# A window-attention and linear-attention kernel: chunks of 128 tokens in time order instead of 112, the image kept by rows

## The chip, the cores and the metric

The kernel runs on one NeuronCore of a Trainium2 chip. The metric is the device time of one execution in microseconds. Before the change it is 1951.62 us, the median of three runs (1951.55 to 1955.96). A profile of one execution stands beside it: every instruction with its start, its duration and what it waited for.

## What is computed

The input is a batch of 16 images of 56 x 56 positions and 128 channels, in fp32. It passes through three layers, each added to its input; the reference, cut to what matters:

```python
# layer 0: attention inside shifted windows of 7 x 7, 4 heads of 32 channels
x = roll(groupnorm(x), (-3, -3));  q, k, v = split(x @ w_qkv);  windows of 49 tokens
attn = softmax(q @ k.T * scale + bias + mask);  x = x0 + roll((attn @ v) @ w_out + b_out, (3, 3))
# layer 1: linear attention over the 3136 tokens of an image in order of time
q, k, v = split(layernorm(t) @ W.T + b);  q = elu(q) + 1;  k = elu(k) + 1
num = einsum('bti,btij->btj', q, cumsum(k[..., None] * v))
den = einsum('bti,bti->bt', q, cumsum(k));   t = t + num / (den + 1e-6)
# layer 2: batch norm of layernorm(t) @ W.T over all 16 images, then a recurrence along the tokens
y = sigmoid(wx_t + y @ V.T);   t = t + y
```

The sum over earlier tokens in layer 1 is computed by chunks: inside a chunk by a masked product of queries and keys (`A`), across chunks by a running state of 128 x 129 (keys by values, with a column of ones for the denominator).

## The kernel before

**Order of the work.** The first part of the program, layers 0 and 1, is written as a list of steps. Each has an engine, an assumed cost, a rank, the steps that it follows, and the buffers that it takes and drops (class `Plan`, lines 58 to 207). When the program is built, the planner plays the list against the assumed costs, first by rank and then up to thirty times by latest start, keeps the best and emits the steps in order of their planned starts. Each engine then executes its own instructions strictly in the emitted order. The numbers of buffers of each kind stand in the dictionary at line 433: three PSUM banks `b`, two pairs of banks `a`, two each of `xn`, `xnT`, `f0`, `f1` and `k`, one `A`, three `state`.

**Tiling.** Tokens lie on partitions in chunks of two image rows, `CH` = 112 tokens; an image has `NCH` = 28 chunks, worked on in `NG` = 7 groups of `G` = 4. Because the windows are shifted by three columns, a row is stored in shifted order: columns 3 to 50, then 51 to 55, then 0 to 2 (`ROW_PIECES`). A load or a store of a group therefore is six DMAs on SyncE's queue (lines 269 and 908), and the causal mask comes from the host in the permuted order of time.

**Layer 0.** `turned` (line 542) loads the groups of one image and transposes them to channels on partitions (L540). ScalarE copies the result into `xw_buf`, where each window's 49 tokens lie together (L567); VectorE takes the statistics (L577). A small chain gives the normalised weights `ws` (L598 to L628; L633 is its last product, once an image). `window_row` (line 672) handles a row of eight windows, eight of them an image: projections of queries and keys (L686) and values (L713) straight from `xw_buf`, scores (L737), softmax on VectorE, GpSimd and ScalarE (L748 to L782), transposes (L792), the product with the values (L811), and ScalarE's copy into `oT_buf` (L832), in token order with shifted rows.

**Layer 1.** `token_group` (line 927) handles a group of four chunks: bias (L937, GpSimd), output projection of layer 0 (L949), addition (L958), layer norm (L871 on VectorE, L878 to L890 on GpSimd), transposes (L540) and copy (L978), features of keys and queries (L991, then L1001, L1010 on ScalarE and L1014 on VectorE), values (L1035, L1044), transposed keys (L1058, L1062), products of keys and queries (L1072) with the mask (L1082). For each chunk follow the products with the state (L1101) and with `A` (L1104), the state's update (L1112) and its copy (L1124). Then come the division and addition (L1172 to L1179), the store (L918), a second layer norm, and the input of the recurrence (L1195, L1199), with batch statistics (L1202) and a copy into `staged` (L1210). `staged` is written to DRAM by sixteen DMAs an image (line 1231).

**Layer 2.** The last part runs the recurrence for 28 segments of 112 steps in parallel, 128 lanes of channels and 16 images, after a warm-up of 16 steps (L1438, L1450, L1453), transposes the results (L1487), adds the layer's input (L1496) and stores the output (L1502). Its inputs come back from DRAM in blocks of eight steps; the last image's part is copied from `staged` by GpSimd (L303). The change leaves this part as it is, apart from that copy.

Of the kernel before, what the change touches and what calls it, by code (L numbers as in the profile page):

```python
# [9 lines left out]
F32 = mybir.dt.float32  # L10
# [4 lines left out]
WS = 7  # L15
# [3 lines left out]

ROW_PIECES = ((0, 3, 48), (48, 51, 5), (53, 0, 3))
# [188 lines left out]
def tile_conv_attn_hybrid(  # L211
# [24 lines left out]
    NCH = T // CH  # L236
    G = 4
    NG = NCH // G
# [24 lines left out]
    xw_bufs = [hold.tile([P, NU, NW, 64], F32, name=f"xw_buf{i}") for i in range(2)]  # L263
    oT_buf0 = hold.tile([P, NU, NW, 64], F32, name="oT_buf0")
# [4 lines left out]
    def load_pieces(b, xt, c0, c1, engines):  # L269

        part = x[b].rearrange("(c r) w ch -> r w c ch", r=2)
        i = 0
        for r in range(2):
            for j, col, n in ROW_PIECES:
                engines[i % len(engines)].dma_start(
                    xt[W * r + j : W * r + j + n, c0:c1], part[r, col : col + n, c0:c1]
                )
                i += 1

    def time_cuts(t0):  # L280

        if t0 < 0:
            return ((0, W + t0, -t0), (-t0, 0, KB + t0))
        return ((0, t0, KB),)
# [10 lines left out]
    def last_xs(to, m):  # L295

        part = to.rearrange("p n c -> p (n c)").rearrange(
            "p (b k n) -> p b k n", b=B, k=KB
        )[:, B - 1]
        row, t0 = divmod(m, W // KB)  # L300
        t0 = KB * t0 - DISP
        for k0, p0, n in time_cuts(t0):
            nc.gpsimd.tensor_copy(  # L303
                part[:, k0 : k0 + n], staged[:, W * row + p0 : W * row + p0 + n, :]
            )
# [30 lines left out]

    FIRST = ((0, G), (G, 3 * G), (3 * G, NCH))
    for c0, c1 in FIRST:
        load_pieces(0, xt_bufs[0], c0, c1, (nc.sync, nc.scalar))
# [14 lines left out]
    bout_sb = constant("bout_sb", [CH, C], b_out.partition_broadcast(CH))  # L354
    awT_sb = constant("awT_sb", [P, 3 * P], attn_wT)
    bqk_sb = constant("bqk_sb", [P, 2], attn_b[0 : 2 * C].rearrange("(i p) -> p i", p=P))
    bv_sb = constant("bv_sb", [CH, C], attn_b[2 * C : 3 * C].partition_broadcast(CH))
    fwT_sb = constant("fwT_sb", [P, P], ffn_wT)
    causal_sb = constant("causal_sb", [CH, CH], causal)
# [10 lines left out]
    with ExitStack() as s1:  # L370
# [40 lines left out]

        q_bufs = []
# [6 lines left out]
        for i in range(2):  # L419
            vb = keep.tile([CH, G, C + 1], F32, name=f"v_buf{i}")  # L420
# [4 lines left out]

        nc.gpsimd.memset(xw_bufs[0][..., WT:], 0.0)
# [3 lines left out]
            xw_bufs[1].rearrange("p u w k -> p (u w k)")[:, 0 : PADQ * CH * C // P],  # L430
# [16 lines left out]
                "xnT": 2,  # L447
                "xfT": 1,
                "r": 1,
                "f0": 2,  # L450
# [1205 lines left out]
```

## Time and profile before

| | |
|---|---|
| median of three runs | 1951.62 us |
| the profiled execution, time | 1951.62 us |
| its span, first to last instruction | 1949.8 us |
| granted TensorE clock, mean over the span | 0.988 |
| last matmul of layers 0 and 1 (L1199) starts at | 1745.8 us |
| DMA: packets, bytes | 164993, 161.25 MB |
| packets under 512 B | 20001 |

The profile names TensorE's matmuls PE and its weight loads PEld (they overlap), VectorE DVE, ScalarE ACT, GpSimd POOL and SyncE SP. L686 is line 686 of the kernel; in the changed kernel lines have other numbers. A matmul in fp32 is two records in the trace (a transpose is one). Durations of matmuls overlap, since they are pipelined, so their sum isn't the time that they take; the distance from one start to the next is nearer to it. "Idle before" of an instruction is the time in which its engine stood still ahead of it, and the releaser is what ended last before it started.

### The profile page before, as it was taken

To read this page: it belongs to the slowest core of one execution; us is meant where nothing else is said; L and a number is where in the kernel's file an instruction comes from. 1 tells how busy PE (TensorE), PEld (TensorE's weight loads), DVE (VectorE), ACT (ScalarE), POOL (GpSimd) and SP (SyncE) were. 2 spreads that over 40 slices of the span, in tenths; PEclk is the share of its full clock that TensorE was granted. 3 is DMA by queue.
4 is the path that set the end of the run, shared out by engine and by line. 5 is a ranking of instruction groups with operands and counts; after the bars stand their busy time and mean duration, and the time that the engine had idled before them with its cause. 6 is when DMAs were issued, how large, how long until landed. Compare 5 with 4: busy or idle time off the path is not lost.

```text
span 1949.8 us, 68357 instructions
## 1 busy us (share of the span) xinstructions
PE 1866.5 (96%) x27854; PEld 1547.4 (79%) x27854; DVE 1370.3 (70%) x3243; ACT 1267.5 (65%) x2755; POOL 1192.9 (61%) x1992
## 2 busy tenths in 40 slices
PE   5999999999999999999999999999999999989787
PEld 4788888888888888888888878888888888767676
DVE  4767767676777767677677677766777767668677
ACT  3767666666666666666766667666766666547455
POOL 5767758676666768576766667676867656640000
PEclk9999999999999999999999999999999999989889
DMA  4112111121212121111212121212111121545998
GB/s 128 33 35 64 26 46 53 40 61 33 64 35 68 26 68 35 55 36 40 64 31 69 37 62 28 68 33 64 31 50 35 29 75 35 198 150 198 413 400 292
DMA packets 164993, 161.25 MB, mean 83 GB/s; under 512 B 20001, under 2 KB 148737, under 8 KB 162881
## 3 DMA queue, kind: packets, MB, share of 16 engines
q1 hardware_dynamic: 163032, 156.02, 25.1%
q8 instruction: 221, 3.62, 0.8%
q10 hardware_dynamic: 1640, 0.80, 0.2%
q14 instruction: 100, 0.81, 0.2%
HBM read 80.38 MB, written 76.38 MB: 80 GB/s over the span
## 4 chain that ended last, share of the span: by engine, by line
PE 82%; DVE 6%; DMA 5%; ACT 3%; issue 2%; POOL 2%; SPq 0%; DVEq 0%; POOLq 0%; ACTq 0%
PE bank L991 9%; PE bank L686 8%; PE bank L540 6%; PE bank L713 6%; PE state_bank L1112 5%; PE pair L737 5%; PE pair L1101 5%; PE bank L1035 5%; PE pair L1104 5%; PE pair L792 5%; PE bank L949 5%; PE pair L811 4%; PE bank L1072 4%; PE bank L1199 4%; DMA out_dram<-o_a 3%; PE bank L1058 2%
## 5 line engine op out<-in xcount | busy, mean ns | idle before, releaser
L782 POOL TENSOR_TENSOR p_buf<-p_buf,rc 128x784 f32<-128x784 f32 x128 | 194.4, 1519 | 127.0 <-DVE rc L779 83.7
L763 POOL TENSOR_TENSOR s<-s,mx 128x784 f32<-128x784 f32 x128 | 192.3, 1502 | 96.0 <-DVE mx L760 89.1
L686 PE MATMUL bank<-xw_buf,ws 128*128 128x392 f32 x512 | 215.2, 507 | 3.8 <-ACT xw_buf L567 1.4
L991 PE MATMUL bank<-xnT,awc_sb 128*128 128x448 f32 x448 | 210.0, 551 | 2.4 <-DVE xt_buf L958 0.7
L1001 ACT ACTIVATE r<-bank,bqk_neg 128x448 f32<-128x448 f32 x224 | 142.2, 635 | 102.6 <-PE bank L991 81.4
L1014 DVE SCALAR_TENSOR_TENSOR f<-bank,bqk_one,r 128x448 f32<-128x448 f32 x224 | 150.3, 671 | 65.3 <-ACT r L1010 64.6
L748 DVE TENSOR_TENSOR s<-pair,wmask_sb 128x784 f32<-128x784 f32 x128 | 123.7, 966 | 87.4 <-PE pair L737 77.7
L1112 PE MATMUL state_bank<-v_buf,k 112*128 112x129 f32 x864 | 174.0, 283 | 2.4 <-ACT k L1062 1.9
L1104 PE MATMUL pair<-v_buf,A 112*112 112x129 f32 x896 | 172.8, 273 | 0.2
L1124 ACT COPY state<-state_bank 128x129 f32<-128x129 f32 x432 | 117.5, 272 | 82.5 <-PE state_bank L1112 77.5
L1101 PE MATMUL pair<-state,f 128*112 128x129 f32 x864 | 169.8, 278 | 0.0
L1112 PEld LDWEIGHTS state_bank<-v_buf,k 112*128 112x128 f32 x864 | 137.6, 190 | 39.4 <-issue 18.3
L1101 PEld LDWEIGHTS pair<-state,f 128*112 128x112 f32 x864 | 129.9, 176 | 46.4 <-issue 35.2
L937 POOL TENSOR_TENSOR xt_buf<-xt_buf,bout_sb 112x512 f32<-112x512 f32 x112 | 141.8, 1279 | 18.2 <-DMA awT_sb<-in_attn_wT_dram 11.2
L777 DVE TENSOR_REDUCE sm<-p_buf 128x16 f32<-128x784 f32 x128 | 122.9, 960 | 41.3 <-ACT p_buf L773 40.5
L802 ACT COPY pT<-pair 128x904 f32<-128x904 f32 x128 | 118.0, 922 | 48.3 <-PE pair L792 44.9
L1453 ACT ACTIVATE y_a<-z_buf,bsh 128x224 f32<-128x224 f32 x224 | 100.1, 447 | 67.5 <-PE z_buf L1450 66.6
L713 PE MATMUL bank<-ws,xw_buf 128*128 128x128 f32 x1024 | 137.6, 277 | 0.0
L713 PEld LDWEIGHTS bank<-ws,xw_buf 128*128 128x128 f32 x1024 | 126.1, 191 | 10.1 <-issue 5.6
L1010 ACT ACTIVATE r<-r 128x448 f32<-128x448 f32 x224 | 130.3, 582 | 2.7
L1179 DVE SCALAR_TENSOR_TENSOR xt_buf<-pair,rd,xt_buf 112x128 f32<-112x128 f32 x448 | 125.5, 342 | 7.3 <-POOL lrs_a L884 0.5
L1104 PEld LDWEIGHTS pair<-v_buf,A 112*112 112x112 f32 x896 | 128.8, 177 | 1.5 <-DVE A L1082 0.8
(143 smaller groups left out, 4897.2 us busy)
## 6 DMA issues: line engine op xcount, KB each, us to landing
out_dram<-o_a SPq DMA_DIRECT2D x13, 1792.0 KB
x_d<-xt_buf SPq DMA_DIRECT2D x224, 96.0 KB
xt_buf<-in_x_dram SPq DMA_DIRECT2D x211, 96.0 KB
xs_d<-staged SPq DMA_DIRECT2D x180, 112.0 KB
xw_buf<-x_d SPq DMA_DIRECT2D x8, 2048.0 KB
spare<-xs_d SPq DMA_DIRECT2D x4, 1680.0 KB
oT_buf<-x_d SPq DMA_DIRECT2D x3, 2048.0 KB
xs_ring<-xs_d SPq DMA_DIRECT2D x3, 1680.0 KB
```

What stands on the lines that cost most here:

```text
L686: nc.tensor.matmul(d[key], o["ws"][:, j * P : (j + 1) * P], xk, start=True, stop=True)
L713: nc.tensor.matmul(d["pv"][:, w2, :], o["xw"][:, u, 2 * w2 : 2 * w2 + 2, :].rearrange("p w k -> p (w k)"), o["ws"][:, 2 * P : 3 * P], star ...
L763: nc.gpsimd.tensor_tensor(d["sf"], d["sf"], d["mx"].unsqueeze(2).to_broadcast([P, nb, WT]), ALU.subtract,)
L782: nc.gpsimd.tensor_tensor(prf, prf, d["rc"].unsqueeze(2).to_broadcast([P, nb, WT]), ALU.mult)
L937: nc.gpsimd.tensor_tensor(t["xt"][:, sl, :], t["xt"][:, sl, :], bout_sb.unsqueeze(1).to_broadcast([CH, G, C]), ALU.add,)
L991: nc.tensor.matmul(d[f"p{j}"], awc_sb[:, j * P : (j + 1) * P], d["xnT"].rearrange("p c t -> p (c t)"), start=True, stop=True,)
L1001: nc.scalar.activation(d[f"r{j}"], d[f"p{j}"], AF.Relu, bias=bqk_neg[:, j : j + 1], scale=-1.0,)
L1010: nc.scalar.activation(d[f"r{j}"], d[f"r{j}"], AF.Exp, scale=-1.0)
L1014: nc.vector.scalar_tensor_tensor(d[key].rearrange("p c t -> p (c t)"), d[f"p{j}"], bqk_one[:, j : j + 1], d[f"r{j}"], ALU.add, ALU.max,)
L1101: nc.tensor.matmul(to, d["f0"][:, cc, :], t["states"][c], start=True, stop=False)
L1104: nc.tensor.matmul(to, d["A"][:, cc, :], v1[:, cc, :], start=c == 0, stop=True)
L1112: nc.tensor.matmul(t["pd"], d["k"][:, cc, :], v1[:, cc, :], start=c == 0, stop=True, skip_group_check=True,)
```

## The change

- Chunks are 128 tokens in plain time order, 24 of them and one of 64. There are still seven groups: six of four chunks, and one with the chunk of 64. The recurrence keeps its 28 segments of 112 steps.
- A group's load or store is one DMA over 128 partitions; the write of `staged` is one DMA an image instead of sixteen. The causal mask is made on GpSimd.
- The image on channels is kept by rows, unshifted, 59 columns by 59 rows: ScalarE copies whole rows and the cut pieces at a group's ends, and GpSimd repeats the first three columns and rows at the far sides (`again`).
- VectorE copies each row of windows from there into one of two small buffers (`gather_windows`), and the projections read that. The second of them lies in the unused end of `oT_buf`.
- The attention's output is written unshifted, so ScalarE cuts the last window of each row in two (`mix_out`: four pieces for a row of windows, eight for the one that wraps, where there were two and four). The copy into `staged` is cut where segments of 112 begin.
- `xnT`, `f0` and `f1` have one buffer instead of two. The assumed costs of the steps are set for the new sizes, and the projections L949 of successive groups are put in order.

The diff, cut to its core (line numbers left out; a line of "..." stands for what is left out):

```diff
+    CK = P
     G = 4
-    NG = NCH // G
+    GT = G * CK
+    GROUPS = [(t0, [CK] * G) for t0 in range(0, T - GT + 1, GT)]
+    GROUPS.append((T // GT * GT, [T % GT]))
+    NG = len(GROUPS)
+    SIDE = H + DISP
...
+    def load_group(b, xt, g, engine):
+        engine.dma_start(
+            chunks_of(g, xt), tokens_of(g, x[b].rearrange("h w c -> (h w) c"))
+        )
...
-    FIRST = ((0, G), (G, 3 * G), (3 * G, NCH))
-    for c0, c1 in FIRST:
-        load_pieces(0, xt_bufs[0], c0, c1, (nc.sync, nc.scalar))
+    for g in range(NG):
+        load_group(0, xt_bufs[0], g, nc.scalar if g % 2 else nc.sync)
...
-                "xnT": 2,
+                "xnT": 1,
...
-                "f0": 2,
-                "f1": 2,
+                "f0": 1,
+                "f1": 1,
...
                 def copy(g=g):
...
+                    xw = image_rows(xw_buf)
+                    t0, t1 = group_tokens(g)
+                    at = t0
+                    while at < t1:
+                        y, c = divmod(at, W)
+                        m = 0 if c else (t1 - at) // W
+                        n = m * W if m else min(W - c, t1 - at)
+                        src = o[g][:, at - t0 : at - t0 + n]
+                        if m:
+                            src = src.rearrange("p (y c) -> p y c", y=m)
+                            nc.scalar.copy(xw[:, y : y + m, 0:W], src)
+                        else:
+                            nc.scalar.copy(xw[:, y, c : c + n], src)
+                        at += n
...
+            def again():
+                xw = image_rows(xw_buf)
+                nc.gpsimd.tensor_copy(xw[:, 0:H, W:SIDE], xw[:, 0:H, 0:DISP])
+                nc.gpsimd.tensor_copy(xw[:, H:SIDE, :], xw[:, 0:DISP, :])
...
+            def gather_windows():
+                y = DISP + WS * u
+                d["xk"] = x_bufs[i % 2]
+                nc.vector.tensor_copy(
+                    d["xk"][:, :, 0:WT].rearrange("p w (i j) -> p w i j", i=WS),
+                    image_rows(xw_buf)[:, y : y + WS, DISP:SIDE].rearrange(
+                        "p i (w j) -> p w i j", w=NW
+                    ),
+                )
...
-                    for i0, y0, m in row_parts(u):
-                        nc.scalar.activation(
-                            rows[:, par, :, y0 : y0 + m],
-                            src[:, :, i0 : i0 + m],
-                            AF.Identity,
-                            bias=o["bias"][:, 2:3],
-                        )
+                    for i0, y0, m in row_parts(u):
+                        at, ys = slice(i0, i0 + m), slice(y0, y0 + m)
+                        pieces = [(rows[:, 0, :, ys], src[:, :, at])]
+                        if par:
+                            cut = WS - DISP
+                            pieces = [
+                                (rows[:, 1, 0:last, ys], src[:, 0:last, at]),
+                                (rows[:, 1, last, ys, 0:cut], src[:, last, at, 0:cut]),
+                                (first[:, ys, 0:DISP], src[:, last, at, cut:WS]),
+                            ]
+                        for to, piece in pieces:
+                            nc.scalar.activation(
+                                to, piece, AF.Identity, bias=o["bias"][:, 2:3]
+                            )
...
+            xk = st("DVE", (0.45, 0.53), rank, gather_windows, [*taken, last_value[i % 2]], drops=[xw_buf])
-            pq = st("PE", (0.67, 0.83), rank, lambda: proj(0, "pq", bq), [*normed, last_score[i % 2]], takes=[bq])
+            pq = st("PE", (0.67, 0.83), rank, lambda: proj(0, "pq", bq), [xk, *normed, last_score[i % 2]], takes=[bq])
...
             def project():
-                d["po"] = bank(bo, CH, G, C)
-                oTf = t["oT"].rearrange("p y w -> p (y w)")
-                for cc in range(G):
-                    c = G * g + cc
+                d["po"] = bank(bo, np, nk, C)
+                for cc in range(nk):
                     nc.tensor.matmul(
                         d["po"][:, cc, :],
-                        oTf[:, c * CH : (c + 1) * CH],
+                        t["oT"][:, t0 + np * cc : t0 + np * (cc + 1)],
                         wout_sb,
                         start=True,
                         stop=True,
                     )
...
+            if g < NG - 1:
+                s = st("PE", (0.44, 0.61), rank, turn_k, [fk], takes=[bk], drops=[bfk])
+                ko = st("ACT", (0.48, 0.59), rank, k_out, [s], takes=[k], drops=[bk])
...
             def xs_out():
...
-                nc.scalar.copy(
-                    t["xsT"][:, :, sl], d["pw"].rearrange("p c j -> p j c")
-                )
+                at = t0
+                while at < t1:
+                    n, j = divmod(at, CH)
+                    m = 0 if j else (t1 - at) // CH
+                    size = m * CH if m else min(CH - j, t1 - at)
+                    src = d["pw"][:, at - t0 : at - t0 + size]
+                    if m:
+                        to = t["xsT"][:, :, n : n + m]
+                        src = src.rearrange("p (n j) -> p j n", n=m)
+                    else:
+                        to = t["xsT"][:, j : j + size, n]
+                    nc.scalar.copy(to, src)
+                    at += size
...
-                for r in range(2):
-                    for m in range(W // KB):
-
-                        for k0, p0, n in time_cuts(KB * m - DISP):
-                            nc.sync.dma_start(
-                                xs_d[r * (W // KB) + m, :, b, k0 : k0 + n, :],
-                                t["xsT"][:, W * r + p0 : W * r + p0 + n, :],
-                            )
+                nc.sync.dma_start(
+                    xs_d[:, :, b].rearrange("m p k n -> p m (k n)"),
+                    t["xsT"].rearrange("p (m k) n -> p m (k n)", k=KB),
+                )
```

## The prediction

> **What bounds the kernel now.** I read the page first, then the busy time by stretches of the span, then who TensorE waited for, then TensorE's instructions in order of time. The page and the stretches:
>
> ```profile
> span 1949.8 us, 68357 instructions
> PE 1866.5 (96%) x27854; PEld 1547.4 (79%) x27854; DVE 1370.3 (70%) x3243; ACT 1267.5 (65%) x2755; POOL 1192.9 (61%) x1992
> ...
> PEclk9999999999999999999999999999999999989889
> ```
>
> ```profile
> 20.00:50.00 30.00, 22.06 (x342) 16.50 (x343) 13.65 (x26) 11.78 (x25) 18.57 (x19) 1.00 0.37 112
> ...
> 1150.00:1250.00 100.00, 98.87 (x1631) 83.06 (x1633) 72.61 (x177) 68.55 (x148) 71.48 (x116) 1.00 0.17 49
> ...
> 1800.00:1850.00 50.00, 37.66 (x222) 32.08 (x220) 33.57 (x56) 25.27 (x57) 1.31 (x4) 0.90 1.02 412
> ```
>
> The columns are length, then busy PE, PEld, DVE, ACT, POOL, granted clock, DMA share, GB/s. Three stages show. Until about 29 us the first image is loaded and normalised. From there to 1746 us (the last L1199 starts at 1745.8) the sixteen images go through attention and linear attention: TensorE is busy 98 to 99% at clock 1.00, the others near 70%, the DMAs at 17%. The last 204 us are the recurrence, where the output's DMAs are full; its instructions are the same in the changed kernel. So the middle stage decides, and the question there is whether "99% busy" means no slack. The waits of TensorE between 400 and 1600 us say yes:
>
> ```profile
> PE state_bank L1112 <- ACT k L1062: 1.2, 2, 0.8
> PE bank L540 <- DVE gst L577: 1.0, 2, 0.6
> PE bank L686 <- DVE v_buf L1044: 0.9, 1, 0.9
> ```
>
> These are the three longest of a list that sums to some 13 us in 1200. TensorE waits for nobody: the stage lasts as long as its instructions take to issue. One image takes (1598.9 - 426.7)/11 = 106.6 us, by the starts of L633, which runs once an image. What one step costs is the distance from its start to the next start, not its duration (durations overlap):
>
> ```profile
> 660.59 0.92 PE L991 MATMUL bank<-xnT,awc_sb 128*128 128x448 f32 x2
> 661.34 0.38 PE L1101 MATMUL pair<-state,f 128*112 128x129 f32 x2
> 661.56 0.39 PE L1104 MATMUL pair<-v_buf,A 112*112 112x129 f32 x2
> 661.78 0.60 PE L1058 MATMUL bank<-ident,f 128*112 128x128 f32 x4
> 662.22 1.06 PE L713 MATMUL bank<-ws,xw_buf 128*128 128x128 f32 x8
> 663.11 0.94 PE L792 MATMUL pair<-ident,p_buf 113*128 113x113 f32 x8
> 663.89 0.40 PE L1112 MATMUL state_bank<-v_buf,k 112*128 112x129 f32 x2
> 664.12 1.04 PE L949 MATMUL bank<-wout_sb,oT_buf 128*112 128x128 f32 x8
> 665.00 0.55 PE L540 MATMUL bank<-ident,xn 112*128 112x112 f32 x4
> 665.38 0.95 PE L1072 MATMUL bank<-f,f 128*112 128x112 f32 x8
> 666.17 0.40 PE L1112 MATMUL state_bank<-v_buf,k 112*128 112x129 f32 x2
> ```
>
> L991 takes 0.75 us; one L1101, L1104 or L1112 takes 0.22; a step of four takes 0.44 (L1058), 0.89 (L713), 0.88 (L949, and L1035 likewise at 672.30), 0.38 (L540), 0.79 (L1072). The cost goes with the columns of the moving operand: 128 columns cost 0.22 whether the stationary operand has 112 (L949) or 128 (L713).
>
> **TensorE's work, step by step.** An image has 3136 tokens: 28 chunks of 112 before, 24 of 128 and one of 64 after. Where the tokens are the moving operand, the columns stay 3136 and the cost stays: L991 and L1199 7 x 0.755 = 5.29 against 6 x 0.863 + 0.12 = 5.30 each; the three transposes 7 x 0.385 = 2.70 against 6 x 0.44 + 0.06; L1072 5.50 against 5.45. Where the chunk is stationary or summed over, each chunk pays its own 128 or 129 moving columns, and three chunks fewer pay (per image):
> - L949 and L1035: 28 x 0.2195 = 6.15 to 24 x 0.2225 + 0.22 = 5.56, -0.59 each
> - L1058: four fewer (the last chunk leaves no state), -0.44
> - L1101 and L1104: three fewer of each, -1.32; L1112: three fewer, -0.67
>
> The sum is -3.61 us. The chunk of 64 brings some eight steps of 0.06 to 0.2 us of its own; for switching to them I add 0.2. So -3.4 us an image, -54.6 us in all. The instruction order of the changed kernel has these counts: 384 + 16 of L949's kind, 384 of L1112's.
>
> Here a rule speaks against the change. The Trainium skill, "TensorE: Matmul & The Clock Gate", section "LDWEIGHTS (loading the stationary operand)", says that a weight load takes its columns divided by 1.2 GHz, and its Part 3 ("What overlaps and what doesn't") that a load overlaps running matmuls only in other row groups. By that the wider chunk would lengthen each of 120 matmuls an image (project, values, products, attends) by two loads of 16 more columns, 2 x 13.3 ns: 3.2 us, nearly all of the gain. The rows say otherwise: 0.2225 against 0.2195, 3 ns; and the L540 transposes, with 128 stationary columns, follow each other every 95 ns, which is less than the rule's 107 for the load alone. I take the rows.
>
> **What moves to the other engines** (per image, the busy shares of the stretch above times 106.6 us as the base):
> - VectorE gathers the windows, 8 copies of 392 columns. The trace has no such copy. The nearest row is L1551, 448 columns contiguous, 382 ns; at the rate of L1561 (432 columns, two inputs, 597 ns) it would be 0.56. So 2.8 to 4.5 us; I take 0.45 each, 3.6. Fewer chunks give back 3 x 0.342 (L1179), 6 x 0.277 (L871) and about 0.9 (L958, L1044): -3.6. Below nothing it can't go. VectorE stays at 76 us.
> - ScalarE writes the image by rows (19 pieces, not 14), the staged inputs (18, not 7) and the attention's output (36, not 18): 34 more instructions for the same columns. L567's rows, 224 ns for 56 columns and 536 for 392, give 172 ns for an empty piece; in sequence pieces overlap, and two of 392 and 56 together took 0.59, so about 0.06. That is 2.0 to 5.8 us, less 3 x 0.272 (L1124) and 0.585 (L1062): +0.6 to +4.4 on 73. I take +2.5, since most pieces follow one another directly.
> - GpSimd copies the wrapped rows and columns (0.6 to 0.7 by L303, 224 columns 0.37), and saves about 3.2 on the small group's L937, L890 and L884: 72 us.
> - SyncE issues one DMA where there were six (L275, L918; six took 2.73 us) and one for the sixteen pieces of an image's staged inputs. Its queue was waiting for VectorE most of the time anyway: nothing.
>
> At 103 us an image all three stand at 70 to 75% beside TensorE, so I cost them at nothing but the waits that they cause. Cover: about 27 us an image of free time on each. What can be late is a hand-over in a full queue. TensorE's waits were about 1.2 us an image; I add 0.25 for a busier ScalarE and for the gather ahead of each row's projections: +4 us (bounds 0 and 25).
>
> Three buffers go from two to one (xnT, f0, f1). f0 is held until a group's last attend, so the next group's maximum (L1014), products (L1072) and mask (L1082) follow it in series: 0.74 + 0.89 + 0.69 and hops, 2.7 us, behind attends of about 2.8 us. That is 5.5 of 14.7 us a group. In the changed order TensorE has 4.4 us of other work (median, priced as above) between a last attend and the next products, and under 1 us in 2 of 111 cases. Nothing is late there.
>
> At the start, 18 issues of 0.64 to 0.76 us on two queues become 7, all of them over 128 partitions, and the last group is small. Stage one ends with GpSimd's seven L937 from 17.5 to 26.9 us ahead of the small power; with their bias earlier it may end up to 6 us sooner, or 1 us later by the wrap copy. I take -3. The end, where the small group follows the last full one through a chain of 9 us: +1.
>
> Sum: 1949.8 - 54.6 + 4 - 3 + 1 = 1897.2 us span, and with the 1.8 us outside the span 1899 us. The profiled execution's 1951.62 is the median itself.
>
> **Rivals.**
> - *ScalarE is late* (0.13): its 34 pieces cost the full 172 ns and land ahead of copies that free TensorE's three PSUM banks. For: three banks, and L567 and L1210 hold one through all pieces. Against: 75% is no bound. Waits of 2 to 3.5 us an image, 1915 to 1945, say 1925.
> - *The weight load is the pace* (0.03): the rule above; 0.2 to 0.4 us an image stay, about 1946, no change.
> - *Slower: the single f0 buffer* (0.05). Place: from the last L1104 through L1014 and L1072 to the next L1104. It decides if VectorE's and TensorE's queues add so much that TensorE stands over 0.5 us in each of 112 hand-overs (112 x 0.5 eats the gain); at 0.8 us it gives about 1899 + 85 = 1985. Against it the 4.4 us of cover.
>
> **How the numbers follow.** The likeliest case (0.79) is 1899 us, from 1885 (no added waits, start -6, the small chunk's switching free) to 1913. The range 1885 to 1922 takes in half of the ScalarE case. Under 0.3% (5.9 us) a measurement of this kernel can't tell from no change. Faster by more: 0.79 + 0.13 = 0.92; within: 0.03; slower: 0.05.
>
> **What would show it.** Right: L633's starts 103 us apart; L949's kind at 0.89 per four with 400 in all; TensorE's waits under 2 us an image; ScalarE under 76% in the middle stage; the last 204 us unchanged. Wrong: waits of TensorE on L1014's successor or on the pieces of L567 and L1210, or a step of 128-column chunks above 0.95.

## The result and the profile after

The changed kernel takes 1936.38 us (median of 4 runs, 1933.64 to 1937.03) against 1953.40 for the kernel before on the same chip (1951.55 to 1955.96). The ratio is 0.9909, 95% interval 0.9892 to 0.9927. That is 17 us less, where the prediction had 52.6 us less: the sign was right, the time lies 14 us above the range. The profiled execution of the changed kernel took 1933.64 us; two lines of its page and the busy time by stretches of it:

```profile
span 1931.8 us, 65226 instructions
PE 1846.2 (96%) x27070; PEld 1489.0 (77%) x27070; DVE 1401.3 (73%) x3227; ACT 1306.1 (68%) x3235; POOL 1159.8 (60%) x2025
```

```profile
20.00:50.00 30.00, 26.85 (x485) 19.37 (x486) 19.39 (x32) 17.45 (x44) 14.89 (x15) 0.87 0.19 53
1150.00:1250.00 100.00, 97.94 (x1646) 78.94 (x1645) 74.01 (x176) 69.61 (x175) 69.84 (x121) 1.00 0.16 49
1800.00:1850.00 50.00, 37.56 (x227) 31.97 (x226) 34.35 (x58) 25.49 (x57) 1.49 (x4) 0.91 1.02 410
```

The first stretch is fuller (26.85 us of TensorE instead of 22.06): the first window projection starts at 24.2 us instead of 30.3. The recurrence is as it was (204.1 us from the last start of L1309, which makes its input, to the end; before 204.0 from L1199). In the middle TensorE is still nearly always busy, ScalarE is at 70%, but TensorE's share is 97.94, not 98.87. An image takes (1582.8 - 532.5)/10 = 105.0 us by the starts of L692, before (1598.4 - 535.3)/10 = 106.3 by L633; 103 was predicted. Whom TensorE waited for between 400 and 1600 us, the three longest:

```profile
PE bank L562 <- DVE v_buf L1151: 3.4, 2, 3.0
PE state_bank L1220 <- ACT state L1232: 1.6, 3, 0.9
PE bank L1142 <- ACT staged L1329: 1.3, 2, 0.7
```

In these 1200 us TensorE is idle for 21.3 us, before for 13.1 (1200 less the busy time). One wait of 3.0 us on VectorE leads the list; before, nothing was over 0.9. The next view is TensorE in order of time, as the prediction read it: what counts is the distance to the next start.

```profile
656.25 1.06 PE L1142 MATMUL bank<-awc_sb,xnT 128*128 128x128 f32 x8
657.14 0.39 PE L1209 MATMUL pair<-state,f 128*128 128x129 f32 x2
...
661.58 0.40 PE L1220 MATMUL state_bank<-v_buf,k 128*128 128x129 f32 x2
661.90 0.43 PE L1054 MATMUL bank<-wout_sb,oT_buf 128*64 128x128 f32 x2
662.27 0.66 PE L562 MATMUL bank<-ident,xn 128*128 128x128 f32 x4
662.76 1.06 PE L1180 MATMUL bank<-f,f 128*128 128x128 f32 x8
663.65 0.39 PE L1220 MATMUL state_bank<-v_buf,k 128*128 128x129 f32 x2
...
689.56 0.43 PE L1209 MATMUL pair<-state,f 128*64 128x129 f32 x2
689.92 0.43 PE L1212 MATMUL pair<-v_buf,A 64*64 64x129 f32 x2
690.29 1.16 PE L784 MATMUL bank<-ws,x_buf 128*128 128x128 f32 x8
```

A full group's step is what the prediction said: L1142 and L1180 0.89 us for four chunks. The chunk of 64 isn't. Its projection (L1054) takes 0.37 us and its two attends 0.36 and 0.37, where 0.22 was taken for each; in the medians over all images its values take 0.36 (0.22 taken), its products 0.26 (0.11), each transpose 0.20 (0.06), each feature 0.17 (0.12). The steps beside it pay too: L1220 ahead of L1054 takes 0.32 us instead of 0.22, the four transposes (L562) behind it 0.49 instead of 0.44.

To split the whole middle stage I take the distance from each TensorE instruction to the next, group the pairs by line, shape and whether the same line follows, and call the median times the count the **spacing**; what exceeds the median by more than 60 ns is summed as **waits**. Before: spacing 1547.7, waits 99.7 us. After: 1515.7 and 121.0. So the spacing fell by 32.0 (predicted 54.6), and the waits grew by 21.3 (predicted 4; that this equals the idle time above is chance).

These waits are more than idle time. Where a full-width step stands next to one whose stationary operand has 64 rows or columns, the distance is about 0.1 us over its median: 177 times in the changed kernel, 17.3 us together, and never before, where no operand is 64 wide. Beside the steps of the attention's heads (32*49 and 49*32) the same happens some 400 times in either kernel, 40 us. So most of the growth in waits also stands beside the chunk of 64.

### The profile page after: what moved, and what is told of

Read it like the earlier page. It is cut to its first block, busy times and chain, and to the rows that moved or that the text cites. A ratio compares the mean times of both kernels' runs of the same rounds, so it can differ in the third digit from the quotient of the medians.

```text
span 1931.8 us, 65226 instructions
## 1 busy us (share of the span) xinstructions
PE 1846.2 (96%) x27070; PEld 1489.0 (77%) x27070; DVE 1401.3 (73%) x3227; ACT 1306.1 (68%) x3235; POOL 1159.8 (60%) x2025
## 4 chain that ended last, share of the span: by engine, by line
PE 77%; DVE 8%; ACT 5%; DMA 4%; issue 2%; POOL 2%; SPq 0%; ACTq 0%; DVEq 0%; POOLq 0%
PE bank L757 8%; PE bank L1095 8%; PE bank L784 6%; PE bank L562 6%; PE pair L808 5%; PE pair L863 5%; PE state_bank L1220 5%; PE bank L1054 5%; PE bank L1180 5%; PE pair L1209 4%; PE bank L1142 4%; PE pair L1212 4%; PE pair L882 4%; PE bank L1309 4%; DMA out_dram<-o_a 4%
## 5 line engine op out<-in xcount | busy, mean ns | idle before, releaser
L1095 PE MATMUL bank<-xnT,awc_sb 128*128 128x512 f32 (+1 forms) x448 | 210.9, 554 | 2.6 <-ACT xnT L1082 0.9
L1105 ACT ACTIVATE r<-bank,bqk_neg 128x512 f32<-128x512 f32 (+1 forms) x224 | 143.6, 641 | 89.3 <-PE bank L1095 69.8
L1118 DVE SCALAR_TENSOR_TENSOR f<-bank,bqk_one,r 128x512 f32<-128x512 f32 (+1 forms) x224 | 149.9, 669 | 44.3 <-ACT r L1114 36.8
L917 ACT ACTIVATE oT_buf<-pair,gbias 128x28 f32<-128x28 f32 (+4 forms) x576 | 144.1, 354 | 30.6 <-PE pair L882 30.1
L1209 PEld LDWEIGHTS pair<-state,f 128*128 128x128 f32 (+1 forms) x768 | 121.9, 188 | 48.9 <-issue 29.3
L1220 PE MATMUL state_bank<-v_buf,k 128*128 128x129 f32 x768 | 156.4, 285 | 2.1 <-ACT state L1232 1.7
L1220 PEld LDWEIGHTS state_bank<-v_buf,k 128*128 128x128 f32 x768 | 122.4, 190 | 44.2 <-issue 22.2
L1212 PE MATMUL pair<-v_buf,A 128*128 128x129 f32 (+1 forms) x800 | 155.9, 276 | 0.1
L1209 PE MATMUL pair<-state,f 128*128 128x129 f32 (+1 forms) x768 | 153.5, 281 | 0.3 <-ACT state L1232 0.2
L1232 ACT COPY state<-state_bank 128x129 f32<-128x129 f32 x384 | 107.4, 280 | 58.8 <-PE state_bank L1220 54.6
L1044 POOL TENSOR_TENSOR xt_buf<-xt_buf,bout_sb 128x512 f32<-128x512 f32 (+1 forms) x112 | 128.3, 1159 | 30.0 <-PE bank L562 25.9
L848 DVE TENSOR_REDUCE sm<-p_buf 128x16 f32<-128x784 f32 x128 | 122.9, 960 | 26.6 <-ACT p_buf L844 25.8
L562 PE MATMUL bank<-ident,xn 128*128 128x128 f32 (+1 forms) x800 | 125.3, 275 | 11.4 <-POOL xn L978 4.0
L1114 ACT ACTIVATE r<-r 128x512 f32<-128x512 f32 (+1 forms) x224 | 130.8, 584 | 3.0
L1565 PE MATMUL z_buf<-y_a,fvT_sb 128*128 128x224 f32 x444 | 127.3, 370 | 0.2 <-ACT y_a L1568 0.2
## 6 DMA issues: line engine op xcount, KB each, us to landing
xw_buf<-x_d SPq DMA_DIRECT2D x8, 2048.0 KB, 22.6
oT_buf<-x_d SPq DMA_DIRECT2D x3, 2048.0 KB, 24.2
```

Of the source, the lines that this page charges most:

```text
L562: nc.tensor.transpose(pt[:, n * cc : n * (cc + 1)], xg[:, cc, :], ident[:n, :n])
L917: nc.scalar.activation(to, piece, AF.Identity, bias=o["bias"][:, 2:3])
L1095: nc.tensor.matmul(d[f"p{j}"], awc_sb[:, j * P : (j + 1) * P], d["xnT"], start=True, stop=True,)
L1105: nc.scalar.activation(d[f"r{j}"], d[f"p{j}"], AF.Relu, bias=bqk_neg[:, j : j + 1], scale=-1.0,)
L1118: nc.vector.scalar_tensor_tensor(d[key], d[f"p{j}"], bqk_one[:, j : j + 1], d[f"r{j}"], ALU.add, ALU.max,)
L1209: nc.tensor.matmul(to, chunk(d["f0"], cc), t["states"][c], start=True, stop=False)
```

## The experiments

The theory after the traces had two parts. First, the chunk of 64 costs far more than its share of columns. Second, VectorE's gather, a copy of 392 columns, is stretched when GpSimd works. This is VectorE and GpSimd with the longest copy, in order of time, and TensorE's instruction that came late:

```profile
477.53 4.83 DVE L747 COPY x_buf<-xw_buf 128x392 f32<-128x392 f32 x1
477.59 1.51 POOL L853 TENSOR_TENSOR p_buf<-p_buf,rc 128x784 f32<-128x784 f32 x1
479.06 0.39 POOL L978 TENSOR_TENSOR xn<-xt_buf,lrs_f 64x128 f32<-64x128 f32 x1
479.42 1.50 POOL L834 TENSOR_TENSOR s<-s,mx 128x784 f32<-128x784 f32 x1
480.88 1.26 POOL L1044 TENSOR_TENSOR xt_buf<-xt_buf,bout_sb 128x512 f32<-128x512 f32 x1
482.28 0.68 DVE L1151 TENSOR_TENSOR v_buf<-bank,bv_sb 128x512 f32<-128x512 f32 x1
483.11 0.34 PE L562 MATMUL bank<-ident,xn 64*128 64x64 f32 x1 [2.96 <-DVE v_buf L1151]
```

A copy that is not stretched takes 0.30 to 0.37 us; this one lasts as long as GpSimd's four instructions follow one another, L1151 stands behind it on VectorE, and TensorE stands for 2.96 us. Over the 128 gathers the mean is 0.68 us. 52 of them take over 0.45 us, and in the trace every one of these ends 0.22 to 0.23 us after the end of a GpSimd instruction. The texts below call this the port theory: the copy needs a port to SBUF that GpSimd holds (the source for it stands under "The waits" in the part on the prediction). The rivals were the ones of the prediction (ScalarE's pieces, the single buffers), and that the planner orders by wrong prices. Ratios are against the kernel before, measured beside each variant (medians of 1952.4 to 1954.0). There is no number 4: two buffers each for `xnT`, `f0` and `f1`, as before, don't fit in SBUF beside the new tiles.

### 1. The gather without the copy

```diff
-                nc.vector.tensor_copy(
+                nc.vector.tensor_reduce(
                     d["xk"][:, :, 0:WT].rearrange("p w (i j) -> p w i j", i=WS),
...
-                    ),
+                    ).unsqueeze(4),
+                    AX.X,
+                    ALU.max,
```

> The changed kernel, with the gather of the windows issued as a tensor_reduce over a last axis of length one instead of a tensor_copy; the same data, the same place in the order of every engine. Port theory: the copy is stretched from 0.30 us to up to 4.8 us whenever GpSimd's tensor_tensor runs, some 43 us of VectorE time in all, and what is queued behind it on VectorE comes late for TensorE; the reduce takes a steady 0.45 to 0.6 us, no gather takes over 1 us, and the time falls by 10 to 20 us, to 1916 to 1926. Rivals (ScalarE's cut pieces, the planner's prices or the single buffers make the waits): the mean gather is hardly shorter than the copies' 0.68 us, the time stays at 1933 to 1940.

Measured: 1923.95 us, ratio 0.9837 (0.9817 to 0.9858), 12.4 less than the changed kernel. All 128 gathers take 0.50 to 0.565 us. The same place in time, in this kernel:

```profile
476.16 1.52 POOL L855 TENSOR_TENSOR p_buf<-p_buf,rc 128x784 f32<-128x784 f32 x1
476.64 0.55 DVE L747 TENSOR_REDUCE x_buf<-xw_buf 128x392 f32<-128x392 f32 x1
```

The reduce runs its 0.55 us inside the same GpSimd instruction that stopped the copy. What that did to TensorE is in the stretch from 477 to 489 us, first of the changed kernel, then of this one (columns as above):

```profile
477.00:489.00 12.00, 8.75 (x132) 6.62 (x130) 9.72 (x9) 5.31 (x14) 6.65 (x6) 0.72 0.09 27
```

```profile
477.00:489.00 12.00, 12.00 (x206) 10.41 (x206) 9.03 (x18) 9.80 (x25) 8.38 (x12) 1.00 0.48 160
```

With the copy TensorE is busy for 8.75 of 12 us at a granted clock of 0.72 in the mean (0.50 from 482.0 to 488.8 us, that is until 5.7 us after the stand); with the reduce it is 12.00 at 1.00. An instruction that is slower alone (0.55 against 0.37) is the cheaper one.

### 2. The short chunk at full width

The stationary operands of the last chunk get 128 columns, so that every instruction, its place and the prices stay; only shapes differ.

```diff
-                        t["oT"][:, t0 + np * cc : t0 + np * (cc + 1)],
+                        t["oT"][:, t0 + np * cc : t0 + np * cc + P],
...
-                        chunk(d["xnT"], cc),
+                        padded(d["xnT_all"], cc),
...
-                    to, d["A"][:, cc, :], v1[:np, cc, :], start=c == 0, stop=True
+                    to, d["A"][:, cc, :], v1[:, cc, :], start=c == 0, stop=True
```

> The changed kernel, with the matmuls of the image's last chunk of 64 tokens given stationary operands of 128 columns (columns 64 to 127 hold what an earlier group left and make rows of output that nobody reads; the masked scores get 128 rows, the lower 64 of them zero). Same instructions, same order. Theory that TensorE pays for a 64-wide stationary operand: project, values, products and the two of attention, five steps an image, fall from 0.26 to 0.36 us to 0.22 us or less, 0.6 us an image, 10 us in all: 1924 to 1929. Rival, that a short chunk costs what any step costs however wide it is: unchanged, 1933 to 1940.

Measured: 1919.84 us, ratio 0.9824 (0.9804 to 0.9844): 16.5 less, more than expected. The short chunk's projection in this kernel's order of time:

```profile
657.95 0.39 PE L1056 MATMUL bank<-wout_sb,oT_buf 128*128 128x128 f32 x2
658.17 0.60 PE L563 MATMUL bank<-ident,xn 128*128 128x128 f32 x4
```

0.22 us instead of 0.37, for twice the columns. The spacing falls by 10.8 us, as expected, and the waits by another 4.1: those beside 64-wide steps fall from 17.3 to 7.3 us, and others grow.

### 3. The old chunk size in the new kernel

```diff
-    CK = P
+    CK = 112
...
-    GROUPS.append((T // GT * GT, [T % GT]))
```

> The changed kernel, but with 28 chunks of 112 tokens in time order, in seven groups of four, and no chunk of 64; the planner gets the prices of the kernel before for these groups. The image kept by rows, VectorE's gather, the merged DMAs and the cut pieces of ScalarE stay. Theory that the larger chunks gave their gain (32 us of TensorE time by the start-to-start times) and the gather and the cuts took 17 of it: 1955 to 1970, slower than the kernel before. Rival, that the chunk size itself is worth little because the 64-token chunk eats what the others save: 1938 to 1947, before less the 6 us of the quicker start and a few more.

Measured: 1951.18 us, ratio 0.9987 (0.9976 to 0.9998). Neither: between the two. Spacing 1549.7, as before; waits 100.2, as before. I read this as the other parts of the change being worth nothing, which experiment 8 corrected: two effects cancel in it.

### 5. Both together, and 13, the transposes too

Kernel 5 is 1 and 2 in one. Kernel 13 also turns the short chunk over all 128 rows (the lower 64 cleared once, or left from an earlier group).

```diff
-                    pt[:, n * cc : n * (cc + 1)], xg[:, cc, :], ident[:n, :n]
+                nc.tensor.transpose(pt[:, P * cc : P * (cc + 1)], xg[:, cc, :], ident)
```

> The gather as a reduce and the padded operands together, on the changed kernel. If the two costs lie one after the other on TensorE's path, the gains add up: 1936.4 - 12.4 - 16.5 = 1907.5, so 1904 to 1911. If both remove the same waits (a stretched copy only matters because the short chunk's steps leave TensorE nothing to do), the gain is hardly more than the larger of the two: 1914 to 1920.

> The reduce and the padded operands (1907.2 us), and the three transposes of the short chunk over all 128 rows as well; the lower 64 rows give columns that nobody reads. Theory that a matmul over 64 rows waits for the array like one with 64 columns: a transpose falls from 0.20 to 0.11 us, 48 of them, 4.5 us: 1901 to 1905. Rival, that 0.20 us is what a step of a single transpose takes: 1906 to 1911.

Measured: 1907.16 us (ratio 0.9768, 0.9747 to 0.9789) and 1900.93 us (0.9726, 0.9698 to 0.9754). The two costs add up, and 64 rows are dear too. A single short transpose in kernel 13:

```profile
659.24 0.27 PE L564 MATMUL bank<-ident,xn 128*128 128x128 f32 x1
659.35 0.82 PE L764 MATMUL bank<-oT_buf,ws 128*128 128x392 f32 x2
```

0.11 us instead of 0.20. This version leaves nothing out and is 53 us under the kernel before. Its spacing is 46.6 us less and its waits are 2.0 more, where the prediction had 54.6 less and 4 more.

### 6. The short group's work left out, and 14, with the reduce

```diff
             n = f"{b}_{g}"
...
+            if g == NG - 1:
+                store(b, g, t, turned_x, xt_buf, rank)
+                return None, None, None
```

> The changed kernel, which leaves out the token work of the last 64 tokens of each image (projection, both layer scales, features, values, attention, batch statistics); they are still loaded, turned and stored as they came. So the time is that of 24 chunks. Theory by the start-to-start times (2.45 us an image on TensorE, with 0.36 us for each 64-wide step, 39 us, and about 10 us of waits with it): 1884 to 1897. Rival, the prices that the prediction took (1.6 us an image, 26 us, no waits): 1907 to 1912.

> The changed kernel with the gather as a reduce, which leaves out the token work of the last 64 tokens of each image as before. Theory that the waits of TensorE beyond the stretched copies come with the short group, and not with chunks of 128 as such: its waits (99 us with stretched copies) fall to those of 28 chunks with the reduce, 83 to 90 us, and the time to 1849 to 1854. Rival, that chunks of 128 leave the other engines too little cover: waits stay at 95 or more, 1860 to 1866.

Besides the work of the 64 tokens these kernels leave out the state's update and copy after the last full chunk, which nothing else reads (16 x 0.225 = 3.6 us of spacing).

Measured: 1863.76 us (ratio 0.9543, 0.9522 to 0.9563) and 1859.81 us (0.9527, 0.9514 to 0.9540). So 64 of 3136 tokens, 2% of the work, cost 72.6 us or 3.7% of the time, far more than even my theory said: 45.9 us of spacing and 22.6 of waits, 14.9 of these beside 64-wide steps (17.3 less the 2.4 that the transposition of x still brings). With the reduce they cost 64.1. Kernel 14 has 94.8 us of waits: nearer to its rival than to its theory. Of the reduce's gain only 4.0 us are left without the short group, though kernel 6 has more stretched copies (66 over 0.45 us). That isn't the short chunk's doing alone, since with 28 chunks of 112 the reduce gives 16.2 us (experiment 8): what a stretched copy costs depends on what stands behind it.

### 7. Other prices for the planner

```diff
-            xk = st("DVE", (0.45, 0.53), rank, gather_windows, [*taken, last_value[i % 2]], drops=[xw_buf])
+            xk = st("DVE", (0.68, 0.76), rank, gather_windows, [*taken, last_value[i % 2]], drops=[xw_buf])
...
-                part(g, (0.88, 1.04), (0.22, 0.38)),
+                part(g, (0.88, 1.04), (0.36, 0.52)),
```

> The changed kernel; only the prices that the planner orders the steps by are other: the gather 0.68 us on VectorE instead of 0.45, and the short chunk's TensorE steps as the trace has them (project and values 0.36, products 0.26, attention 0.72, features and whole 0.17, transposes 0.20). Same instructions, another order. Theory that the engines are really busy for that time: 1930 to 1942. Rival, that the order made from wrong prices causes the waits of 21 us: 1915 to 1926.

Measured: 1936.24 us, ratio 0.9914 (0.9889 to 0.9940): no change, waits 122.7. The order made from wrong prices isn't the cause.

### 8. 28 chunks of 112 with the reduce, and 12, with many DMAs

Kernel 8 is 1 and 3 in one. Kernel 12 adds nearly the number of DMAs of the kernel before:

```diff
-            engine.dma_start(
-                chunks_of(g, xt), tokens_of(g, x[b].rearrange("h w c -> (h w) c"))
-            )
+        for p0, p1 in CUTS if b else ((0, 112),):
+            engine.dma_start(to[p0:p1], src[p0:p1])
```

> The 28 chunks of 112 tokens with the gather as a reduce. Its copies stretch as in the changed kernel (0.76 us in the mean), but its waits on TensorE sum to what they did before the change. Theory that a stretched copy only costs where TensorE has caught up with VectorE: little to gain, 1946 to 1951. Rival, that the shared port costs the same 12 us wherever the gather stands: 1937 to 1941.

> The 28 chunks of 112 with the gather as a reduce (1935.0 us, 13 us of TensorE's waits less than the kernel before), but with every load and store of a group from the second image on in six DMAs by partitions, and an image's staged inputs in fourteen, as the kernel before has them in number; the planner gets that kernel's prices for SyncE. Theory that SyncE's queue never held anybody: 1932 to 1939. Rival, that the many DMAs (their issue on SyncE, and late loads) made the 13 us of waits: 1944 to 1950.

Measured: 1935.03 us (ratio 0.9908, 0.9887 to 0.9929) and 1935.93 us (0.9902, 0.9877 to 0.9928). My theory that a stretched copy costs only where TensorE has caught up fell: the reduce gives 16.2 us here. Without any change of the chunk, then, the kernel has the whole measured gain of the change. Spacing 1549.4, waits 86.4: 13 us under the kernel before, which kernel 3 lost again to stretched copies (0.76 us in the mean). The number of DMAs has no part in it.

### 9. The rest spread over two groups

```diff
-    GROUPS = [(t0, [CK] * G) for t0 in range(0, T - GT + 1, GT)]
-    GROUPS.append((T // GT * GT, [T % GT]))
+    GROUPS = [(GT * g, [CK] * G) for g in range(FULL)]
+    GROUPS += [(GT * FULL + 288 * g, [96] * 3) for g in range(2)]
```

> The changed kernel with the gather as a reduce, and the image cut into five groups of four chunks of 128 and two of three chunks of 96 (26 chunks, still seven groups) instead of six of four and one of one chunk of 64. No padding. By the runs so far 28 chunks of 112 take 1935 us with the reduce, and 24 of 128 without the last 64 tokens about 1863.8 - 12.4 = 1851, some 1861 if the 64 tokens lay in them: 18 us for each chunk more. Theory that only a width of 64 is dear, and a group too small to cover its own waits: 26 chunks give 1861 + 2 x 18 = 1897, so 1890 to 1906. Rival, that every operand under 112 columns pays 0.14 us a step: six chunks with about six such steps, 80 us an execution, over 1960.

Measured: 1925.81 us, ratio 0.9864 (0.9843 to 0.9886): both wrong. The rival fell: with 96 columns an instruction follows the other after 0.109 us, as with 112, so 96 isn't dear. But my 1897 rested on kernel 6, whose 64 tokens are missing altogether. It also took 12.4 us for the reduce there, where kernel 14 shows 4.0. By the spacing (1514.4, that is 1549.4 less 17.5 us for each of the two chunks saved) the count was right; the waits, 114.3 instead of 86.4, ate the rest, and none of them stands beside a 64-wide step.

### 10 and 11. No gather, and ScalarE's output in fewer pieces

```diff
-            xk = st("DVE", (0.45, 0.53), rank, gather_windows, [*taken, last_value[i % 2]], drops=[xw_buf])
+            gather_windows()
+            xk = st("DVE", 0.01, rank, lambda: None, [*taken, last_value[i % 2]], drops=[xw_buf])
```

Here gather_windows only names the tile, whose content stays constant.

> The changed kernel, which leaves out the gather of the windows: the attention's projections and values read a constant in its place, with the same dependencies. So all other instructions and waits stay and only VectorE's 128 copies are gone. Theory that a gather costs the end only by being stretched at the shared port: a little more than the reduce gave, 1917 to 1925. Rival, that its 0.55 us of VectorE time ahead of each row's projections is not hidden either: 1900 to 1914.

Measured: 1922.70 us, ratio 0.9853 (0.9827 to 0.9879), 1.3 us under kernel 1. That is less than this measurement tells apart: a steady gather looks covered, and what the gather costs the end is its stretched copies. The reading has one weakness. The planner was given a price of 0.01 for the step and ordered TensorE's steps otherwise, so more changed than the copies (in kernels 1, 2 and 5 the order is the changed kernel's own).

```diff
-                            cut = WS - DISP
-                            pieces = [
-                                (rows[:, 1, 0:last, ys], src[:, 0:last, at]),
-                                (rows[:, 1, last, ys, 0:cut], src[:, last, at, 0:cut]),
-                                (first[:, ys, 0:DISP], src[:, last, at, cut:WS]),
-                            ]
+                            pieces = [(rows[:, 1, :, ys], src[:, :, at])]
```

> The changed kernel with the attention's output written in 18 instead of 36 ScalarE instructions an image: the odd windows of a row in one piece, so that the last window's three wrapped columns land one row too low. That leaves out the wrap of these columns in the output; all else stays. Theory that ScalarE's pieces are covered: 1931 to 1941. Rival, that the pieces make TensorE wait for PSUM: about 0.17 us for each of 288 instructions, of which a third reaches the end, 1915 to 1927.

Measured: 1941.18 us, ratio 0.9943 (0.9923 to 0.9962): 5 us slower with 288 instructions fewer (waits 127.1). Here too the planner made another order from the lower price, and what that cost isn't separated; but a gain of 9 us or more, as the rival had it, isn't there. So these pieces are not what TensorE waits for.

All kernels beside each other; the spacing and waits are of the middle stage of the profiled execution, the time is the median:

| kernel | time | spacing | waits |
|---|---|---|---|
| before | 1953.4 | 1547.7 | 99.7 |
| after: 24 chunks of 128 and one of 64 | 1936.4 | 1515.7 | 121.0 |
| 1 reduce | 1924.0 | 1515.7 | 110.7 |
| 2 padded | 1919.8 | 1504.9 | 116.9 |
| 5 reduce, padded | 1907.2 | 1505.3 | 103.5 |
| 13 reduce, padded, transposes too | 1900.9 | 1501.1 | 101.7 |
| 3 chunks of 112 | 1951.2 | 1549.7 | 100.2 |
| 8 chunks of 112, reduce | 1935.0 | 1549.4 | 86.4 |
| 9 five groups of 128, two of 96, reduce | 1925.8 | 1514.4 | 114.3 |
| 6 no short group | 1863.8 | 1469.8 | 98.4 |
| 14 no short group, reduce | 1859.8 | 1469.9 | 94.8 |

Spacing and waits are of one execution each. The recurrence behind them, with the same instructions, took 202 to 212 us in these executions, so a few us between two times need not come from the middle stage.

## Why the prediction was wrong, step by step

| term of its sum (us) | predicted | measured |
|---|---|---|
| TensorE's work (spacing) | -54.6 | -32.0 |
| waits of TensorE | +4 | +21.3 |
| start | -3 | -6.1 |
| end | +1 | +0.1 |
| deviations under 60 ns | not in it | -1.3 |
| sum, of the profiled executions | -52.6 | -18.0 |

**The full chunks nearly held.** The prediction's sum without the short chunk's token work is -54.6 - 16 x 1.67 = -81.3 us. Kernel 6 shows 1469.8 - 1547.7 = -77.9, and -74.3 with the state update that it leaves out and the prediction keeps. Of the 7.0 us between, 2.1 are the short chunk's own transposition of x (0.20 us for 0.06); half of the rest is that a step of L949 or L1035 with 128 stationary columns takes 6 ns more than with 112 (0.224 against 0.218), not 3. The rows still decided rightly against the rule that was weighed there, which had 26.6.

**The failed step: "the chunk of 64 brings some eight steps of 0.06 to 0.2 us of its own; for switching to them I add 0.2".** It priced the chunk by its moving columns, 1.67 us an image without x's own transposition, its switching among them. By the spacing the same steps take (45.9 - 3.6)/16 = 2.64, and the steps beside them 17.3/16 = 1.08 more. With x's transposition the chunk was priced at 27.7 us (16 x 1.73) and cost 62.8, which is 35 us, as much as the whole miss (52.6 - 18.0 = 34.6); the other misses cancel. Padding shows that it is the width: in kernel 13 the spacing is 14.6 us less than in kernel 1 and nothing is left beside 64-wide steps, though all waits fall only by 9.0. What padding doesn't give back is that a short step isn't short in proportion (a feature takes 0.17 us with 64 columns, 0.86 with 512).

No trace of before had a 64-wide operand, but it had narrower ones, and the last line that the prediction shows, with the three behind it, has the price of a change of width:

```profile
666.17 0.40 PE L1112 MATMUL state_bank<-v_buf,k 112*128 112x129 f32 x2
666.50 0.95 PE L737 MATMUL pair<-kT,q_buf 32*49 32x49 f32 x64
667.38 1.02 PE L991 MATMUL bank<-xnT,awc_sb 128*128 128x448 f32 x2
668.24 0.38 PE L1101 MATMUL pair<-state,f 128*112 128x129 f32 x2
```

L1112 takes 0.33 us ahead of L737 instead of 0.22, and L991 0.86 behind it instead of 0.75. As an estimate from these rows, seven 64-wide stretches an image (three transposes, L1054, L1142, L1180, and L1209 with L1212), each with a change to and fro at 0.1 us, come to 1.4 us an image where 0.2 was added. With an upper bound from there the range would have been wider.

The Trainium skill has a sentence that bears on the width, in "TensorEngine Tiling (Array Packing)", section "Key Properties": "Mode switching requires drain". It gives no price. By the rows it comes to 0.14 to 0.15 us within a step with 64 columns, to 0.09 within a transpose over 64 rows, to 0.05 to 0.1 in the step on either side, and to nothing for 96 or 112. That the array drains there is that page's explanation; the runs show only that the time goes with the width.

**The waits: "so I cost them at nothing but the waits that they cause", and +4 for those.** Without the 17.3 us beside the short chunk's steps the waits grew by 4.0. That the prediction has the same number is luck: it is the sum of a gain of 13.3 us that it didn't see and of costs in other places and sizes than it had (next paragraph). The cover of 27 us an image was there, and a steady gather looks covered (kernel 10). What failed is the gather's duration: 0.45 us was taken from rows of other instructions, and the copies took 0.30 to 4.83. The Trainium skill, "SBUF — State Buffer", section "Who interferes with whom", says that a copy on VectorE may use a port pair that it shares with GpSimd, that the one who has it locks it for the whole instruction, and that a reduce never takes it. From it and the trace of before an upper bound could have been estimated, one GpSimd instruction of 1.5 us more; the trace after shows even four in a row. The change of the copy alone is shown to cost 12 us; that it is the port is inferred from that page and from where the stretched copies end.

**The waits in one sum.** 99.7 before; -13.3 by the other parts (kernel 8); +8.4 by chunks of 128 (kernel 14 against 8), 2.4 of them beside the transposition of x; +15.9 by the short group (kernel 1 against 14), 14.9 of them beside its 64-wide steps; +10.3 by the stretched copies (after against 1); 121.0 after. Except for the last, these are differences between kernels with different orders of steps, and which pair is taken matters: the copies' part is 3.6 without the short group (6 against 14) and 13.8 with chunks of 112 (3 against 8).

**What was right or didn't matter.** The start gained about what had been its bound, 6 us. The recurrence is unchanged. The rival of a late ScalarE named 1925 us, its range of 1915 to 1945 holds the result, and it is wrong in its cause: kernel 11 takes away 18 of its 34 pieces without a gain, kernel 8 keeps those pieces and has fewer waits than before, and for the others (L606, L1329) the trace shows TensorE idle for 5.6 us in the whole middle stage, before for 4.3 (L567, L1210). The single buffers were not tried by themselves. But in the changed kernel TensorE is idle behind the features' maximum (L1118) for 2.9 us in all, where the rival needed over 0.5 us in each of 112 hand-overs (and its 1899 + 85 is 1984, not 1985).

**What stays open.** Which of the other parts takes 13 us of waits away: not the number of DMAs; ScalarE's copy of the image by whole rows was not tried alone. Why groups of uneven size bring waits even where their chunks are not dear, 28 us with two groups of three chunks of 96 (kernel 9 against 8). And why a stretched copy costs 12 to 16 us in some kernels and 4 in another.

## What to carry to other kernels

A remainder is priced by its own steps, not by its share of the columns. A full chunk's step is no upper bound (0.22 us here against 0.37): look for rows where the width changes, add what the change costs in the steps on both sides, and if no row shows the remainder's width, pad it to one that the rows show. An instruction put on a second engine is covered only if it keeps to the duration that was taken for it; look at which of its neighbours share something with it, and prefer the form with a steady time, even a slower one. When a change of several parts lands near the expected sign, undo parts in pairs: here the chunk size looked worth 15 us in one pair and 11 in the other, and with the remainder mended 34.

## What the runs showed of the hardware that was not expected

- A VectorE copy of 128 x 392 fp32, 0.30 to 0.37 us when it is not stretched, lasted 4.83 us beside four GpSimd instructions in a row; each of the 52 over 0.45 us ended 0.22 to 0.23 us after a GpSimd instruction. The reduce over an axis of one, 0.50 to 0.565 us, was never stretched in 128 of them.
- TensorE's step with a 64-column stationary operand takes 0.36 to 0.37 us, with 128 columns 0.22; a transpose over 64 rows 0.20, over 128 rows 0.11; 96 columns are as quick as 112 (0.109 us for an instruction).
- A full-width step beside a 64-wide one, or beside the heads' 32*49 and 49*32, takes about 0.1 us more, on either side: 0.33 instead of 0.22 for L1112, 0.86 instead of 0.75 for L991. Beside the heads this is 40 us of 1950 in both kernels.
- Where TensorE stood for 3 us, the granted clock was 0.50 for 6.8 us, until 5.7 us after the stand; without the stand, in kernel 1, it was 1.00. Such a wait is paid more than once.
